# An AdaLN transformer block on one core: a weight load cut into four pieces, and six products moved from GpSimd to VectorE

## The chip, the cores and the metric

The kernel runs on one core of a Trainium2 chip. A core has five engines with an instruction queue each, worked off in order: TensorE (PE in the profile), VectorE (DVE), ScalarE (ACT), GpSimd (POOL) and SyncE (SP, which only issues transfers). The metric is the device time of one execution in microseconds; the figure for a kernel is the median of its runs.

## The reference

Two batches of 4096 rows of 512 values pass an attention-like block with a gated scan, and then a feed-forward block whose inputs and weights are rounded to FP4 in blocks of 16.

```python
mod = (silu(c) @ wmod).reshape(B, 6, 1, -1)
sa, ca, ga, sb, cb, gb = mod[:, 0], ..., mod[:, 5]
ga = sign(ga) * maximum(abs(ga), 0.25)          # gb the same
h = layernorm(x) * (1 + ca) + sa
# attention
xn = h / norm(h) * sqrt(512) * gamma
q, kv, a = split(xn @ W_qkva.T, 3);  a = sigmoid(a)
y[t] = a[t] * y[t - 1] + kv[t]                  # scan over the 4096 rows
x = x + ga * q * y
# feed-forward, fp4() rounds in blocks of 16
h = fp4(layernorm(x) * (1 + cb) + sb)
g = silu(h @ fp4(w_gate).T) * (h @ fp4(w_up).T)
x = x + gb * (fp4(g) @ fp4(w_down).T)
```

## The kernel before

**Stages.** The first stage (to about 564 us) is the attention part, the second the feed-forward part. The change lies in the opening of the first: the function `start` and slots 0 and 1 of the loop that follows.

**Tiles.** A token tile g is 128 rows; four of them make a block i of 512 rows. The 16 blocks are worked off in slots: slot = 4*i + e, where e counts the four groups of 128 output columns. In a slot, `mix(i, xT, e)` multiplies the block by the three parts of weight group e (`PARTS` = 2, 1, 0, which are a, kv and q), each in float16 high and low halves, 36 matmuls of 128x512 in all, into three banks of PSUM. Even e use banks 0 to 2 and odd e banks 3 to 5, so mix(0,2) writes the banks that mix(0,0) used. Block 0's first mix goes tile by tile instead, 36 matmuls of 128x128 for each of its four token tiles. The results of slot s are read in slot s+1: `gates` (sigmoid of bank one, on ScalarE), `scan` (VectorE), `read_out` (VectorE), `halves` and a transpose, and two slots later `joined` and `residual`.

**Token tiles.** Tile g goes through `norm_load`, `norm_moments`, `norm_stats` (VectorE, then rstd on GpSimd, L160 and L161), `norm_center` (L166), `norm_shift` (L172), `norm_square` (ScalarE, L354), `norm_gain` (rn on GpSimd, L359 and L361), `norm_hi` (ScalarE, L367) and `norm_lo` (VectorE, L372). `norm_lo` ends with a DMA transpose into xT, issued from SyncE. `start` does this for tiles 0 to 3; slot s does the high and low half of tile s+4 and prepares the next ones.

**Weight groups.** A group e has three parts of 128x512. For each: `load_part` (SyncE, 256 KB), `gamma_qkva` (times gamma, L281), `square_qkva` (sum of squares on ScalarE, L285), `inverse_qkva` (rs: VectorE L288, then a power on GpSimd L289), `hi_qkva` (L308 or L310) and `lo_qkva` (VectorE, L316, and a DMA transpose into wqT, L324). In short, (2,a), (2,b), (2,c) are the parts of group 2 in the order of `PARTS`. `gain_qkva` turns the sums into the gains `us` (L296 and L299). High and low halves of tiles and weights share a ring of four buffers `hl`; each comes free when its transpose has landed.

**Modulation.** Each of the six modulation vectors needs a 1 MB column block of `wmod`. Number 2 (`ga`) is loaded by `load_mod(2)`, multiplied in `mod_columns(2)` on TensorE after mix(0,0), and in slot 1 `signed_floor` (ScalarE L250; VectorE L251 to L253) and `prep_gain` (L563) make from it the factors gq that `read_out` uses.

**Order.** The source order is the order of each engine's queue: a manual schedule covers all engines. An instruction that waits holds up what is behind it on its engine. All loads and transposes of the opening are issued from SyncE, in one order:

```python
norm_lo(1, xT)
load_mod(2)            # one transfer of 1 MB
...
norm_lo(2, xT)         # transpose three
...
norm_lo(3, xT)         # transpose four
load_qkva(2)           # three transfers of 256 KB
```

Of the kernel before, what the change touches and what calls it, by code (L numbers as in the profile page):

```python
# [43 lines left out]
def tile_adaln_block(  # L44
# [165 lines left out]
    def load_mod(s, pieces=1):  # L210
        w = KC // pieces
        for k in range(0, KC, w):
            S.dma_start(
                wm[s][:, k : k + w, :],
                wmod[k * P : (k + w) * P, s * D : (s + 1) * D].rearrange("(k p) e -> p k e", p=P),
            )
# [109 lines left out]
    PARTS = (2, 1, 0)  # L326
# [17 lines left out]
    def norm_center(g):  # L344
        xh[g] = center(xld.pop(g), xstat[g][0], ca[g * P // N])
# [24 lines left out]
    def norm_lo(g, xT):  # L370
        h, rn, hl = xh.pop(g)
        V.scalar_tensor_tensor(  # L372
            out=hl[:, 1, :], in0=h, scalar=rn, in1=hl[:, 0, :], op0=ALU.mult, op1=ALU.subtract
        )
        t = g % KC
        S.dma_start_transpose(xT[:, :, t * P : (t + 1) * P], flat(hl))
# [270 lines left out]
    def start():  # L647
        a, b_, c_ = PARTS

        def load_mod_piece(s, k):  # L650
            S.dma_start(wm[s][:, k, :], wmod[k * P : (k + 1) * P, s * D : (s + 1) * D])

        load_mod(1, KC)
        norm_load(0)
        S.dma_start(gam, gamma.partition_broadcast(P))
        for k, then in enumerate((PARTS[0], PARTS[1], PARTS[2], None)):
            if then is None:
                norm_load(1)
            else:
                load_part(0, then)  # L660
            load_mod_piece(0, k)
        norm_load(2)
        norm_load(3)
        load_qkva(1)
        norm_load(KC)
        pc = mod_spread(1, 0)
        ps = mod_spread(0, 0)
        r1 = mod_rows(1)
        r0 = mod_rows(0)

        norm_moments(0)
        norm_stats(0)
        gamma_qkva(0, a, V)
        A.activation(ca[0], pc, AF.Copy, bias=1.0)
        square_qkva(0, a)
        gamma_qkva(0, b_, V)
        square_qkva(0, b_)
        inverse_qkva(0, a, a + 1)
        norm_center(0)
        gamma_qkva(0, c_, V)  # L680
        inverse_qkva(0, b_, b_ + 1)
        hi_qkva(0, a, True)
        square_qkva(0, c_)
        lo_qkva(0, a)
        inverse_qkva(0, c_, c_ + 1)
        hi_qkva(0, b_, True)
        norm_moments(1)
        norm_stats(1)
        lo_qkva(0, b_)
        A.copy(sa[0], ps)  # L690
        norm_center(1)
        hi_qkva(0, c_, True)
        norm_shift(0)
        norm_square(0)
        lo_qkva(0, c_)
        norm_gain(0, G)
        norm_shift(1)
        norm_square(1)
        norm_hi(0)
        norm_moments(2)  # L700
        norm_moments(3)
        norm_gain(1, G)
        norm_stats(2)
        norm_hi(1)
        norm_stats(3)
        norm_lo(0, xT)
        norm_center(2)
        norm_shift(2)
        norm_square(2)
        norm_lo(1, xT)  # L710
        load_mod(2)
        norm_gain(2, G)
        norm_center(3)
        norm_shift(3)
        norm_square(3)
        norm_gain(3, G)
        norm_hi(2)
        gamma_qkva(1, a, V)
        norm_lo(2, xT)
        norm_hi(3)  # L720
        gamma_qkva(1, b_, V)
        square_qkva(1, a)
        square_qkva(1, b_)
        norm_lo(3, xT)
        load_qkva(2)
        norm_load(KC + 1)
        inverse_qkva(1, b_, a + 1)
        gamma_qkva(1, c_, V)
        mod_store(*r1, tag="yh")
        square_qkva(1, c_)  # L730
        mod_store(*r0)
        hi_qkva(1, a, False)
        inverse_qkva(1, c_, c_ + 1)
        for part in PARTS:
            gamma_qkva(2, part)
        lo_qkva(1, a)
        hi_qkva(1, b_, True)
        norm_moments(KC)
        hi_qkva(1, c_, True)
        lo_qkva(1, b_)  # L740
        norm_stats(KC)
        lo_qkva(1, c_)
        norm_load(KC + 2)
        load_qkva(3)
        norm_center(KC)
        for part in PARTS:
            square_qkva(2, part)
        norm_shift(KC)
        norm_square(KC)
        norm_gain(KC, G)  # L750
        gain_qkva(0)
        norm_moments(KC + 1)
        inverse_qkva(2)
        norm_stats(KC + 1)
        for part in PARTS:
            hi_qkva(2, part, False)
            lo_qkva(2, part)
        gain_qkva(1)
        gain_qkva(2)
# [8 lines left out]
    with order:  # L768
        xT = new_xT()
        start()  # L770
        for slot in range(NS + 3):
            i, e = divmod(slot, KC)
            if e == 0 and slot < NS:
                if slot:
                    xT = nxT
                nxT = new_xT() if i + 1 < NBLK else None
            units, coming = coming, load_units(plan[slot]) if slot < len(plan) else []
            g = slot + KC
            if g + 3 < NT:
                norm_load(g + 3)  # L780
            cur = mix(i, xT, e) if slot < NS else None
            late = rows
            rows = None
            if slot == 0:
                cols = mod_columns(2)
            elif slot in MODS:
                rows = mod_rows(MODS[slot])
            if gate is not None:
                gate = gates(*gate)
            if len(joining) == 2 or slot >= NS + 2:  # L790
                residual(*joined(*joining.pop(0)))
            if g < NT:
                norm_hi(g)
            if gate is not None:
                gate = scan(*gate)
            if slot == 1:
                signed_floor(gq, cols, atile([P, KC, B], F32, "mag"))
                prep_gain(0)
            if g + 2 < NT:
                norm_moments(g + 2)  # L800
            if gate is not None:
                gate = read_out(*gate)
            if g < NT:
                norm_lo(g, nxT)
            if gate is not None:
                joining.append(halves(*gate))
            if slot == 1:
                for part in PARTS:
                    square_qkva(3, part)
            if g + 2 < NT:  # L810
                norm_stats(g + 2)
            for u in units:
                u.advance(1)
            if g + 1 < NT:
                norm_center(g + 1)
            for u in units:
                u.advance(2)
                u.advance(3)
            if g + 1 < NT:
                norm_shift(g + 1)  # L820
                norm_square(g + 1)
            if slot == 1:
                scale_qkva(3)
                for part in PARTS:
                    hi_qkva(3, part, False)
                    lo_qkva(3, part)
            for u in units:
                u.advance(4)
            coming = [Unit(*c_) for c_ in coming]
            for u in coming:  # L830
                u.advance(0)
            if g + 1 < NT:
                norm_gain(g + 1, G)
            if slot == 0:
                for part in PARTS:
                    gamma_qkva(3, part)
            for u in units:
                u.advance(5)
                u.advance(6)
            assert all(u.step == 7 for u in units)  # L840
            if 0 < slot < KC:
                prep_gain(slot)
            if slot + 2 in MODS:
                load_mod(MODS[slot + 2])
            if late is not None:
                mod_store(*late)
            if slot == KC + 1:
                ca[1] = mod_load(1, 1, "mod_c1")
                sa[1] = mod_load(0, 1, "mod_s1")
            if slot == NS // 2 + KC:  # L850
                mods_for(0)
            if slot == NS // 2 + KC + 2:
                gbs[0] = mod_load(5, 0, "mod_gb")
            if slot in (NS - 6, NS - 5):
                for n in range(2):
                    n += 2 * (slot - NS + 6)
                    x1s[n] = load_x1(n)
            if NS - 5 <= slot < NS - 1:
                n = slot - NS + 5
                xst[n] = stats_x(x1s[n])  # L860
                if n in (1, 2):
                    run(quant_x(n - 1, x1s.pop(n - 1), xst.pop(n - 1)))
            gate = cur
# [190 lines left out]
```

## Time and profile before

| | us |
|---|---|
| median of 3 runs (lowest to highest) | 1942.48 (1939.48 to 1942.65) |
| profiled execution, its own time | 1940.56 |
| its span | 1938.8 |
| TensorE busy | 1905.6 |
| VectorE busy | 1603.8 |
| ScalarE busy | 993.3 |
| GpSimd busy | 419.6 |

All times of instructions are from one profiled execution and count from the start of its span; around the span lie 1.8 us more. A line of the timeline gives start, busy time, engine, source line, what is written from what, how many, and in brackets the idle time of the engine ahead of it with what ended it. Starts of queued instructions on VectorE lie closer together than their busy times, since the end of one overlaps with the next. A transfer's row gives the time of its issue, not of its landing.

### The profile page before, as it was taken

To read this page: it belongs to the slowest core of one execution; us is meant where nothing else is said; L and a number is where in the kernel's file an instruction comes from. 1 tells how busy PE (TensorE), PEld (TensorE's weight loads), DVE (VectorE), ACT (ScalarE), POOL (GpSimd) and SP (SyncE) were. 2 spreads that over 40 slices of the span, in tenths; PEclk is the share of its full clock that TensorE was granted. 3 is DMA by queue.
4 is the path that set the end of the run, shared out by engine and by line. 5 is a ranking of instruction groups with operands and counts; after the bars stand their busy time and mean duration, and the time that the engine had idled before them with its cause. 6 is when DMAs were issued, how large, how long until landed. Compare 5 with 4: busy or idle time off the path is not lost.

```text
span 1938.8 us, 25685 instructions
## 1 busy us (share of the span) xinstructions
PE 1905.6 (98%) x9220; PEld 900.1 (46%) x9220; DVE 1603.8 (83%) x2671; ACT 993.3 (51%) x1705; POOL 419.6 (22%) x603
## 2 busy tenths in 40 slices
PE   7799999999999999999999999999999999999999
PEld 4344444444444444444444444444444444444444
DVE  5777889999859988888888888888888888888875
ACT  4544467777755454444445444444454444445432
POOL 4544466666530101000000000001001000000000
PEclk9999999999999999999999999999999999999999
DMA  8697679999833434433433344334434433433343
GB/s 228 157 238 199 170 166 204 220 203 198 189 93 63 94 63 76 81 63 63 80 77 63 67 81 83 63 74 84 68 63 78 79 63 63 82 75 63 61 69 58
DMA packets 483152, 206.66 MB, mean 107 GB/s; under 512 B 439574, under 2 KB 440854, under 8 KB 483024
## 3 DMA queue, kind: packets, MB, share of 16 engines
q1 hardware_dynamic: 468576, 171.50, 41.6%
q0 software_dynamic: 14448, 33.52, 9.8%
q8 instruction: 72, 1.18, 0.2%
q14 instruction: 56, 0.46, 0.1%
HBM read 63.12 MB, written 33.58 MB: 50 GB/s over the span
## 4 chain that ended last, share of the span: by engine, by line
PE 83%; DVE 2%; issue 1%; ACT 1%; DMA 0%; POOL 0%; ACTq 0%; POOLq 0%; DVEq 0%
PE mm L881 45%; PE sd L928 24%; PE mm L393 14%; DMA yt<-yh 0%; POOL xr L443 0%; DVE ld L172 0%; DVE xn L106 0%; DMA out_dram<-xr 0%; DVE xn L122 0%; POOL out_dram L445 0%; DVE y L420 0%; ACT y L435 0%; DVE hl L372 0%; DVE ld L166 0%; DVE hid L901 0%
## 5 line engine op out<-in xcount | busy, mean ns | idle before, releaser
L881 PEld LDWEIGHTS <-x2T 128*128 128x128 f16 x4608 | 450.9, 98 | 469.4 <-issue 1.3
L393 PE MATMUL mm<-xT,wqT 128*128 128x512 f16 (+1 forms) x2412 | 506.1, 373 | 20.4 <-DMA xT<-hl 9.5
L881 PE MATMUL mm<-wuT,x2T 128*128 128x512 f16 (+1 forms) x2304 | 487.7, 361 | 1.0 <-DVE hid L901 1.0
L881 PE MATMUL mm<-wgT,x2T 128*128 128x512 f16 (+1 forms) x2304 | 487.7, 361 | 0.0
L928 PE MATMUL sd<-wdT,hT 128*128 128x512 f16 x2112 | 465.8, 379 | 0.0
L393 PEld LDWEIGHTS <-wqT 128*128 128x128 f16 x2412 | 232.7, 99 | 295.4 <-issue 23.1
L928 PEld LDWEIGHTS <-hT 128*128 128x128 f16 x2112 | 206.6, 98 | 242.7
L896 ACT ACTIVATE silu<-mm,u 128x512 f32<-128x512 f32 (+1 forms) x192 | 125.1, 652 | 286.0 <-PE mm L881 282.4
L901 DVE SCALAR_TENSOR_TENSOR hid<-mm,u,silu 128x512 f32<-128x512 f32 (+1 forms) x192 | 128.5, 673 | 139.5 <-PE mm L881 130.4
L590 POOL TENSOR_SCALAR rstd<-vs 128x1 f32<-128x1 f32 x64 | 13.8, 216 | 983.9 <-ACT sq L588 983.9
L143 ACT ACTIVATE u<-ud,rms 128x1 f32<-128x1 f32 x64 | 19.0, 297 | 277.9 <-DVE rms L139 277.9
L120 ACT ACTIVATE sle<-sl 128x512 f16<-128x512 f32 (+2 forms) x162 | 147.2, 909 | 0.0
L113 ACT ACTIVATE she<-sh 128x1408 bf16<-128x1408 bf16 (+1 forms) x128 | 128.5, 1004 | 4.1
L952 POOL DMA_DIRECT2D out_dram<-o x63 | 56.3, 894 | 270.1 <-DVE o L946 266.2
L411 DVE TENSOR_TENSOR_SCAN y<-sig,cy,mm 128x512 f32<-128x512 f32 x56 | 71.7, 1280 | 46.3 <-ACT sig L405 17.4
L427 ACT COPY yh<-y 128x1024 uint16<-128x1024 uint16 x64 | 67.0, 1047 | 83.3 <-DVE y L420 75.2
L122 DVE SCALAR_TENSOR_TENSOR xn<-hid,xn 128x1408 f32<-128x1408 f32 x64 | 103.6, 1619 | 3.7 <-ACT hid L116 3.7
L106 DVE TENSOR_TENSOR xn<-hid,inv 128x1408 f32<-128x1408 f32 x64 | 104.0, 1625 | 2.2
L125 DVE SCALAR_TENSOR_TENSOR hhl<-hid,xn 128x1408 f16<-128x1408 f32 x64 | 104.0, 1625 | 2.2
L147 DVE TENSOR_REDUCE amh<-hid 128x88 f32<-128x1408 f32 x64 | 103.7, 1620 | 2.2
L116 ACT ACTIVATE hid<-xn 128x1408 f32<-128x1408 f32 x64 | 88.3, 1379 | 30.7 <-DVE xn L106 30.7
L443 POOL TENSOR_TENSOR xr<-xr,y 128x512 f32<-128x512 f32 x64 | 81.3, 1270 | 54.2 <-ACT y L435 52.8
(114 smaller groups left out, 1917.3 us busy)
## 6 DMA issues: line engine op xcount, KB each, us to landing
ld<-out_dram SPq DMA_DIRECT2D x65, 256.0 KB, 2.9
xr<-in_L_attn_x_dram SPq DMA_DIRECT2D x64, 256.0 KB, 3.5
out_dram<-xr POOLq DMA_DIRECT2D x64, 256.0 KB, 3.8
out_dram<-o POOLq DMA_DIRECT2D x63, 256.0 KB, 3.9
ld<-in_L_ffn_w_gate_dram SPq DMA_DIRECT2D x22, 256.0 KB, 3.2
ld<-in_L_ffn_w_up_dram SPq DMA_DIRECT2D x22, 256.0 KB, 3.3
scratch<-in_L_wmod_dram SPq DMA_DIRECT2D x4, 1024.0 KB, 5.5
ld<-in_L_ffn_w_down_dram SPq DMA_DIRECT2D x16, 256.0 KB, 3.2
```

The costliest lines, as they stand in the source:

```text
L106: V.tensor_tensor(blocks(xn), blocks(src), spread(inv, nb), ALU.mult)
L113: A.activation(blocks(she), spread(sh, nb), AF.Copy, scale=WPEAK)
L116: A.activation(a, xn, AF.Abs, scale=MAGIC)
L120: A.activation(blocks(sle), spread(sl, nb), AF.Copy, scale=WPEAK)
L122: V.scalar_tensor_tensor(out=xn, in0=a, scalar=FLOOR, in1=xn, op0=ALU.max, op1=ALU.add)
L125: V.scalar_tensor_tensor(out=nq, in0=a, scalar=FLOOR, in1=xn, op0=ALU.max, op1=ALU.subtract)
L147: V.tensor_reduce(am, src.rearrange("p (b k) -> p b k", k=QB), AX.X, ALU.max, apply_absolute_value=True)
L393: T.matmul(pp[:, t : t + width], wqT[:, wp * KC + k, r * P : (r + 1) * P], xT[:, xp * KC + k, t : t + width], start=n == 0, stop=n == 3 * ...
L881: T.matmul(pp[:, : n1 - n0], x2T[:, xp * KC + k, :], wt[:, wp * KC + k, n0:n1], start=n == 0, stop=n == 3 * KC - 1,)
L896: A.activation(sl[:, :w], pairs[j][0][:, :w], AF.Silu, scale=u[:, 0:1])
L901: V.scalar_tensor_tensor(out=hid[:, n0:n1], in0=pairs[j][1][:, : n1 - n0], scalar=u[:, 1:2], in1=sl[:, : n1 - n0], op0=ALU.mult, op1=ALU.mult,
L928: T.matmul(pd, hT[:, hp * IC + k, :], wdT[:, wd_chunk(wp, k), :], start=n == 0, stop=n == 3 * IC - 1,)
```

## The change

Three things change, all in the opening.

1. The 1 MB load of modulation weight 2 becomes four loads of 256 KB, one after each of the four x transposes; the three loads of weight group 2, which followed transpose four, go one each after transposes two, three and four.
2. The gamma products of group 2 move from GpSimd to VectorE and are put one at a time into VectorE's queue, each with its square on ScalarE; before, three stood together on GpSimd, and the squares stood ahead of `norm_shift` of tile 4.
3. The gamma products of group 3 (slot 0) move from GpSimd to VectorE at the same place in the text; their squares move in slot 1 from behind `halves` to ahead of `scan`.

```diff
--- before.py
+++ after.py
@@ -704,11 +704,13 @@
         norm_hi(1)
         norm_stats(3)
         norm_lo(0, xT)
+        load_mod_piece(2, 0)
         norm_center(2)
         norm_shift(2)
         norm_square(2)
         norm_lo(1, xT)
-        load_mod(2)
+        load_mod_piece(2, 1)
+        load_part(2, a)
         norm_gain(2, G)
         norm_center(3)
         norm_shift(3)
@@ -717,12 +719,15 @@
         norm_hi(2)
         gamma_qkva(1, a, V)
         norm_lo(2, xT)
+        load_mod_piece(2, 2)
+        load_part(2, b_)
         norm_hi(3)
         gamma_qkva(1, b_, V)
         square_qkva(1, a)
         square_qkva(1, b_)
         norm_lo(3, xT)
-        load_qkva(2)
+        load_mod_piece(2, 3)
+        load_part(2, c_)
         norm_load(KC + 1)
         inverse_qkva(1, b_, a + 1)
         gamma_qkva(1, c_, V)
@@ -731,23 +736,25 @@
         mod_store(*r0)
         hi_qkva(1, a, False)
         inverse_qkva(1, c_, c_ + 1)
-        for part in PARTS:
-            gamma_qkva(2, part)
         lo_qkva(1, a)
         hi_qkva(1, b_, True)
         norm_moments(KC)
         hi_qkva(1, c_, True)
         lo_qkva(1, b_)
+        gamma_qkva(2, a, V)
+        square_qkva(2, a)
         norm_stats(KC)
         lo_qkva(1, c_)
         norm_load(KC + 2)
         load_qkva(3)
         norm_center(KC)
-        for part in PARTS:
-            square_qkva(2, part)
+        gamma_qkva(2, b_, V)
+        square_qkva(2, b_)
         norm_shift(KC)
         norm_square(KC)
         norm_gain(KC, G)
+        gamma_qkva(2, c_, V)
+        square_qkva(2, c_)
         gain_qkva(0)
         norm_moments(KC + 1)
         inverse_qkva(2)
@@ -791,6 +798,9 @@
                 residual(*joined(*joining.pop(0)))
             if g < NT:
                 norm_hi(g)
+            if slot == 1:
+                for part in PARTS:
+                    square_qkva(3, part)
             if gate is not None:
                 gate = scan(*gate)
             if slot == 1:
@@ -804,9 +814,6 @@
                 norm_lo(g, nxT)
             if gate is not None:
                 joining.append(halves(*gate))
-            if slot == 1:
-                for part in PARTS:
-                    square_qkva(3, part)
             if g + 2 < NT:
                 norm_stats(g + 2)
             for u in units:
@@ -833,7 +840,7 @@
                 norm_gain(g + 1, G)
             if slot == 0:
                 for part in PARTS:
-                    gamma_qkva(3, part)
+                    gamma_qkva(3, part, V)
             for u in units:
                 u.advance(5)
                 u.advance(6)
```

No matmul, transpose or arithmetic is added or removed; SyncE issues three transfers more.

## The prediction

> **What bounds the kernel now.** I read the page first, then the waits, TensorE's timeline, and the queues of VectorE, GpSimd and SyncE, all between 20 and 90 us.
>
> ```profile
> PE 1905.6 (98%) x9220; PEld 900.1 (46%) x9220; DVE 1603.8 (83%) x2671; ACT 993.3 (51%) x1705; POOL 419.6 (22%) x603
> PE   7799999999999999999999999999999999999999
> ```
>
> TensorE is busy 1905.6 of 1938.8 us, and what is missing lies in the first two slices of 48.5 us. The diff touches only that opening, so what it can win is in TensorE's gaps there.
>
> ```profile
> 60.08 2.75 PE L393 MATMUL mm<-xT,wqT 128*128 128x512 f16 x12 [0.51 <-DVE y L420]
> 68.53 10.49 PE L393 MATMUL mm<-xT,wqT 128*128 128x512 f16 x36 [5.69 <-DMA wqT<-hl]
> 82.02 8.16 PE L393 MATMUL mm<-xT,wqT 128*128 128x512 f16 x37 [3.01 <-DMA xT<-hl]
> ```
>
> From 82.02 on (mix(1,0), slot 4) TensorE has no gap for over 160 us: whatever moves 82.02 moves the end. So the question is what 82.02 waits for. It is the transpose of the last x tile of block 1 (issued 77.60), which follows norm_lo in slot 3, which follows VectorE's queue of slots 2, 1 and the opening. The gap at 68.53 has the same source: the transposes of weight group 3, issued from 65.75, when lo_qkva(3) got its turn on VectorE. So VectorE's in-order queue from 36 to 68 us carries the end:
>
> ```profile
> 36.62 0.74 DVE L166 SCALAR_TENSOR_TENSOR ld<-xr,mv,ca 128x512 f32<-128x512 f32 x1
> 41.95 0.75 DVE L172 SCALAR_TENSOR_TENSOR ld<-ld,rstd,sa 128x512 f32<-128x512 f32 x1 [4.60 <-POOL rstd L161]
> ...
> 46.17 0.49 DVE L310 TENSOR_SCALAR hl<-scratch,rs 128x512 f16<-128x512 f32 x1 [2.57 <-POOL rs L289]
> ...
> 55.86 1.21 DVE L252 TENSOR_SCALAR mag<-mag 128x8 f32<-128x8 f32 x1
> 57.11 1.18 DVE L253 SCALAR_TENSOR_TENSOR gq<-gq,mag 128x8 f32<-128x8 f32 x1
> ...
> 63.31 0.17 DVE L288 TENSOR_SCALAR rs<-us 128x3 f32<-128x3 f32 x1 [1.20 <-ACT sq L285]
> ...
> 68.28 1.22 DVE L411 TENSOR_TENSOR_SCAN y<-sig,mm 128x512 f32<-128x512 f32 x1
> ```
>
> Each bracket is idle time ahead of the instruction and its releaser. GpSimd's queue explains the 4.60:
>
> ```profile
> 36.86 4.08 POOL L281 TENSOR_TENSOR scratch<-scratch,gam 128x512 f32<-128x512 f32 x3 [2.60 <-DMA scratch<-in_L_attn_W_qkva_dram]
> 41.03 0.23 POOL L160 TENSOR_SCALAR rstd<-mv 128x1 f32<-128x1 f32 x1
> ...
> 54.55 3.72 POOL L281 TENSOR_TENSOR scratch<-scratch,gam 128x512 f32<-128x512 f32 x3
> ```
>
> The three gamma products of group 2 wait for their weights until 36.86 and run until 40.94; rstd of tile 4, whose statistics were ready at 34.7, is queued behind them. The weights are late because SyncE's queue is:
>
> ```profile
> 26.60 0.57 SPq L213 DMA_DIRECT2D scratch<-in_L_wmod_dram  x1
> 29.06 4.75 SPq L376 DMA_TRANSPOSE xT<-hl  x2
> 33.86 1.52 SPq L208 DMA_DIRECT2D scratch<-in_L_attn_W_qkva_dram  x3
> ```
>
> Behind the 1 MB load the issue of transpose four took 3.41 us against 1.24 for others, and transpose three landed 6.0 us after its issue, at 35.1, against a shortest 2.7.
>
> **What the Trainium skill says.** "SBUF — State Buffer", Who interferes with whom: a VectorE instruction in a two-port mode, or with two SBUF inputs, contends with a GpSimd instruction that reads SBUF, and the second blocks. The trace agrees: L252 and L253 touch 8 elements and take 1.21 and 1.18 us while GpSimd's gamma products (1.26 each) run; L251, which reads PSUM, takes 0.17. "DMA: Bandwidth & Descriptors", Queues, rings and completion order: descriptors of one issuing queue are consumed in ring order, so a transpose waits for loads ahead of it; the 6.0 us landing fits. "TensorE: Matmul & The Clock Gate", Part 1: idle time halves the clock, by free-running windows of 3.41 us. The granted clock is 0.50 from 33 to 39 us and from 67 to 73, after gaps of 4.88 and 5.69; the gap of 3.01 left it at 1.00.
>
> **The change, part by part.** No matmul changes. Six products of 128x512 go from GpSimd (4.08+3.72 = 7.80 us) to VectorE (0.69 each; 0.61 from start to start). One load becomes four of 256 KB, three more issues of 0.45 us = 1.4 us on SyncE, but the three loads of group 2 now go between the transposes.
>
> SyncE: transposes one and two keep 22.78 and 25.3; transpose three is ready at 29.03 as before, now behind 512 KB, part of it moved. Its landing lies between 31.8 (shortest, 2.7) and 35.1 (as before); I take 33.0 (median 3.9). Transpose four then issues at about 31.25 and ends at 32.5; the last piece and the last part of group 2 at 33.4. That part, issued at 33.0, lands 3.2 us after its issue ends (the median of the six such loads from 20 to 85 us) at 36.6; with a repeat of the 3.41 us stall, 38.8.
>
> VectorE from 34.54 (end of lo_qkva(1,b)), in the new order, with spacings of the rows before:
> - gamma (2,a) 35.15; statistics 35.25; lo (1,c) 35.92. Its hi half needs the buffer that transpose three frees: before 35.15, now 33.0, so the 1.23 us wait goes.
> - center 36.58; gamma (2,b) 37.19; rstd is now ready by 36.3 to 37.1 (GpSimd 0.3+0.6, up to 0.6+1.05, after 35.4); shift ends 37.85, before 42.6.
> - gamma (2,c) 38.46; squares on ScalarE follow, the last ends 39.65 (0.73 to 0.8 each; norm_square goes ahead of it); rs at 39.8; GpSimd's rn, us, rs powers (0.3+0.55+0.85+0.85) from 39.0 to 41.55. hi (2,a) starts at **41.6, before 46.17: 4.6 earlier**. The 4.60 and 1.23 waits are gone, the 2.57 wait for rs stays at some 2, and three products (1.83) are added.
> - To the shift of tile 5 spacing is unchanged (5.87 from 46.17): 47.5. Then three gammas of group 3 to 50.0. Before, scan stood 2.18 after the shift, waiting for sig; now 2.5. Sig is at 49.0, so 0.3 is lost: 4.2 earlier.
> - gq: ScalarE now does three squares (0.81 each) between norm_hi and cy, mag: norm_hi 50.0, squares to 53.1, mag 53.2, L251 at 53.45, before 55.78. VectorE idles 2.1 us here: gain down to 2.3. But L252 and L253 lose their contention: about 0.5 from L251 to prep_gain instead of 2.55. Gain 4.4.
> - The 1.20 us wait for squares at 63.31 is gone; next late is GpSimd, where rs now stands behind rstd until 58.15 (before 62.54). hi (3,a) at 59.05, before 64.45: **5.4 earlier**. Then as before: scan at 62.9, first transpose of group 3 at 60.4, mix(0,3) at 63.2, mix(1,0) at 76.6.
>
> TensorE does not limit this: even at its old 44.81 mix(0,1) ends at 52.74; mix(0,2) needs the bank that read_out frees at about 55.5 and ends near 58.3, before mix(0,3) at 63.2. The idle gap there, 4.9, still costs half clock, but as before it is covered by the wait for xT. SyncE's 1.4 us of issue lie in the stretch where its stall shrinks. GpSimd's loss of 7.8 us of work costs nothing.
>
> Sum: -5.4 us on the profiled execution (1940.56, span 1938.8) gives 1935.2. The median of the runs is 1942.48, 1.9 above the profiled one, inside their 1939.48 to 1942.65; the same -5.4 gives **1937.1**. About 0.2% (3.9 us) is what a measurement of this kernel can tell from no change.
>
> **Rivals.**
> 1. The last part of group 2 comes late: gamma (2,c) blocks VectorE, with shift's successors behind it. The price is landing minus 37.85: 1.0 with one stall of the 3.41 kind (38.8), 2.5 with the slowest landing of such loads, 7.3 us after 33.0. Gain 2.9 to 4.4, some **1939.0**. For it: the opening's loads landed in up to 7.3. Against: less is queued ahead of each transpose.
> 2. The clock falls in the gap before mix(1,0): that costs about 5 us at half clock, 2.5 us (36 matmuls took 10.49 at 68.53 against 7.93 at 44.81). It needs mix(0,3) to end well before xT lands, so a warm start at 63.2; the 4.9 us gap speaks against. **1939.6**.
> 3. The chain is not what I read and the gain goes into another wait (sig or the gq wait of 2.1 growing): **1942.5**, within 0.2%.
> 4. The slow side: every transpose put behind a load pays 2.17 us more issue (3.41-1.24), as transpose four did. Three such before the last part (6.5) bring it to 43.1, eating nearly all 5.4; three more on the transposes of group 1 hold the hl buffers that hi (2,c) and norm_hi(4) need, which adds up to 4: **1946**. It decides from some three stalls on to no gain, five to slower. Against it: transposes behind four loads at 35.95 took 4.67 for three, only 0.95 over.
>
> **How the numbers follow.** Main 0.66 (gain 4 to 7: 1935.5 to 1938.5), first rival 0.14, second 0.09, third 0.05, fourth 0.06. Half of the first counts as faster and half as same, a little of the second faster: faster 0.74, same 0.19, slower 0.07. The range reaches down to 9 gained (5.4, some 1.0 where GpSimd's powers take their short ends, and 2.6 for the spread of the runs, whose lowest lies 3.0 under the median) and up to 1.5 gained (the worse end of the first rival, 2.9, with 1.4 of spread): 1933.5 to 1941.0. It leaves out rivals three and four.
>
> **What would show it.** In the profile after: no GpSimd L281 rows; shift of tile 4 near 38 and hi (2,a) near 41.6; L252 and L253 near 0.2; VectorE waiting about 2 us for mag; mix(0,3) near 63 and mix(1,0) near 76.6. It is wrong if hi (2,a) stays past 45, a gamma (2,c) wait over 2 us appears, or mix(1,0) starts past 80.

## The result, and the profile after

| | before | after |
|---|---|---|
| median of 8 runs each, us (lowest to highest) | 1941.77 (1939.48 to 1942.65) | 1935.99 (1934.53 to 1936.86) |
| ratio to before, 95% interval | | 0.9971, 0.996 to 0.9982 |
| profiled execution, its own time / span | 1940.56 / 1938.8 | 1934.53 / 1932.8 |

The kernel became 5.8 us faster, and the slowest run of after lies 2.6 below the fastest of before. 1937.1 had been forecast, 5.4 below the median of the three runs known then.

On the page of after, the engines' busy times and TensorE's 40 slices:

```profile
PE 1905.7 (99%) x9220; PEld 899.6 (47%) x9220; DVE 1605.6 (83%) x2677; ACT 991.0 (51%) x1705; POOL 415.2 (21%) x597
PE   7899999999999999999999999999999999999999
```

TensorE's work is what it was (1905.7 against 1905.6). Six instructions went from GpSimd to VectorE (603 to 597, 2671 to 2677), and the second slice rose from 7 to 8. So the span lost idle time, most of it in the opening. TensorE's timeline of after from 20 us on (start, busy, line, count, and in brackets the idle time ahead and what ended it) shows how much:

```profile
33.63 2.91 PE L393 MATMUL mm<-xT,wqT 128*128 128x128 f16 x36 [2.92 <-DMA xT<-hl]
...
63.69 10.54 PE L393 MATMUL mm<-xT,wqT 128*128 128x512 f16 x36 [4.66 <-DMA wqT<-hl]
76.92 8.36 PE L393 MATMUL mm<-xT,wqT 128*128 128x512 f16 x38 [2.69 <-DMA xT<-hl]
```

33.63 is the token tile that transpose three brings. mix(0,3) starts at 63.69 where it started at 68.53, and mix(1,0) at 76.92 where it started at 82.02: 5.10 us of the span's 6.0. VectorE's timeline of after tells where the 5.10 was won:

```profile
37.74 0.75 DVE L172 SCALAR_TENSOR_TENSOR ld<-ld,rstd,sa 128x512 f32<-128x512 f32 x1 [0.46 <-POOL rstd L161]
38.99 0.69 DVE L281 TENSOR_TENSOR scratch<-scratch,gam 128x512 f32<-128x512 f32 x1 [0.50 <-DMA scratch<-in_L_attn_W_qkva_dram]
...
42.12 0.49 DVE L310 TENSOR_SCALAR hl<-scratch,rs 128x512 f16<-128x512 f32 x1 [1.34 <-POOL rs L289]
...
54.04 0.17 DVE L251 TENSOR_SCALAR gq<-sd 128x8 f32<-128x8 f32 x1 [2.36 <-ACT mag L250]
54.12 0.16 DVE L252 TENSOR_SCALAR mag<-mag 128x8 f32<-128x8 f32 x1
54.32 0.17 DVE L253 SCALAR_TENSOR_TENSOR gq<-gq,mag 128x8 f32<-128x8 f32 x1
...
59.59 0.49 DVE L310 TENSOR_SCALAR hl<-scratch,rs 128x512 f16<-128x512 f32 x1 [1.00 <-POOL rs L289]
```

Line by line against before: the shift of tile 4 (L172) waits 0.46 us for rstd, no longer 4.60. Gamma (2,c) waits 0.50 for its weights: the new wait that the first rival feared, and small. hi (2,a) starts at 42.12, before 46.17. The wait of 2.36 for mag is new: ScalarE has the three squares of group 3 first. L252 and L253 take 0.16 and 0.17 us where they took 1.21 and 1.18. hi (3,a) starts at 59.59, before 64.45.

The other 0.9 us lie far from the change. Later on the same timeline TensorE has a gap at about 250 us in both kernels. Before had one more at 377.94, in slot 40, here with its bracket:

```profile
377.94 186.64 PE L393 MATMUL mm<-xT,wqT 128*128 128x512 f16 x864 [0.85 <-ACT cy L414]
```

After has none there: its row of 1440 matmuls (576 + 864) runs through it.

```profile
245.68 312.65 PE L393 MATMUL mm<-xT,wqT 128*128 128x512 f16 x1440 [2.31 <-ACT y L435]
```

### The profile page after: what moved, and what is told of

It is laid out like the page before. It is cut to its first block, busy times and chain, and to the rows that moved or that the text cites. A ratio compares the mean times of both kernels' runs of the same rounds, so it can differ in the third digit from the quotient of the medians.

```text
span 1932.8 us, 25689 instructions
## 1 busy us (share of the span) xinstructions
PE 1905.7 (99%) x9220; PEld 899.6 (47%) x9220; DVE 1605.6 (83%) x2677; ACT 991.0 (51%) x1705; POOL 415.2 (21%) x597
## 3 DMA queue, kind: packets, MB, share of 16 engines
q8 instruction: 72, 1.18, 0.3%
## 4 chain that ended last, share of the span: by engine, by line
PE 87%; DVE 0%; issue 0%; ACT 0%; POOL 0%; ACTq 0%
PE mm L888 47%; PE sd L935 24%; PE mm L393 16%; ACT y L435 0%; DVE o L953 0%; DVE o L964 0%; DVE ld L172 0%; DVE st L153 0%; DVE hl L372 0%; DVE y L420 0%; DVE ld L166 0%; DVE hid L908 0%; ACT sig L405 0%; ACT sq L354 0%; DVE inv L100 0%
```

## The experiments

The theory: the gain is VectorE's queue in the opening, as the prediction has it, and comes from parts 2 and 3 (gamma products of group 2, of group 3). Two rivals: that the loads and the earlier transposes (part 1) bring it, and that the contention on L252 and L253 alone does. The first five kernels do parts alone or undo one; s1 moves the loads; b1 and b3 go on to the wait that the change had made; the f kernels test a later gap that turned out to take gains back. Ratios are to before, run on the same chip. Starts of different executions are not exactly comparable: the first x transpose, which stands ahead of everything that the edits move, is issued between 22.03 us (e2) and 22.94 us (b1). The table at the end of this section gives it for each, and where it matters a start is counted from there as well.

### One part alone: e1, e2, e3

e1, part 1 on the kernel before:

```diff
         norm_lo(0, xT)
+        load_mod_piece(2, 0)
...
         norm_lo(1, xT)
-        load_mod(2)
+        load_mod_piece(2, 1)
+        load_part(2, a)
...
         norm_lo(3, xT)
-        load_qkva(2)
+        load_mod_piece(2, 3)
+        load_part(2, c_)
```

> Before, with part 1 of the change alone: the modulation load in pieces and the loads of group 2 between the transposes; all gamma products stay on GpSimd. Theory V (VectorE's queue carries the end, through GpSimd's products): the products start at about 34.4 instead of 36.86, but the last waits for its weights until 39.0, so rstd of tile 4 is free at about 40.4 instead of 41.03; hi (2,a) some 0.7 us earlier, the whole 0.3 to 1.5 us faster. Rival T (the gain is in the x transposes and TensorE's first mix, which the loads release): this part alone gives most of it, 4 us or more.

Measured: 1941.05 against 1940.82, ratio 1.0002 (0.9994 to 1.001). hi (2,a) came at 45.09 where before had 46.17, and mix(1,0) at 81.41 where it had 82.02, of which 0.2 us is left when counted from the first x transpose. The loads alone bring nothing that the times show, less than was expected; slot 40 has a gap of 1.66 where before has 0.85 (the last experiments are about it).

e2, part 2 on the kernel before:

```diff
-        for part in PARTS:
-            gamma_qkva(2, part)
...
         lo_qkva(1, b_)
+        gamma_qkva(2, a, V)
+        square_qkva(2, a)
...
-        for part in PARTS:
-            square_qkva(2, part)
+        gamma_qkva(2, b_, V)
+        square_qkva(2, b_)
...
         norm_gain(KC, G)
+        gamma_qkva(2, c_, V)
+        square_qkva(2, c_)
```

> Before, with the products of group 2 on VectorE, loads as before. Theory V: gamma (2,a) waits for its late weights until 36.9 and (2,b), (2,c) follow without a wait, so hi (2,a) is at about 43.3 (before 46.17, after 42.12); 2.9 us faster than before. L252 and L253 still take 1.2 each. Rival T: about no gain (under 1), since the transposes stay late. Rival C (the gain is the removed contention between the two engines on L252 and L253): no gain.

Measured: 1939.62, ratio 0.9993 (0.9985 to 1.0001), less than half of what was expected. Yet hi (2,a) was at 43.01, 3.2 us earlier, and mix(1,0) on e2's TensorE timeline 3.6 us earlier (2.9 counted from the first x transpose, which is what theory V had):

```profile
78.39 41.83 PE L393 MATMUL mm<-xT,wqT 128*128 128x512 f16 x180 [5.10 <-DMA xT<-hl]
```

The opening did what it should and the end did not follow. The row says why: the same 180 matmuls took 39.13 in before (39.01 in after) and take 41.83 here, after a gap of 5.10. The clock had fallen in the gap, which took 2.8 us back. The view by stretches has it at half behind the gap (stretch, its length, TensorE busy with its matmuls, granted clock, DMA share, GB/s):

```profile
78.00:82.00 4.00, 3.61 (x9) 0.50 0.58 157
```

e3, part 3 on the kernel before:

```diff
+            if slot == 1:
+                for part in PARTS:
+                    square_qkva(3, part)
             if gate is not None:
                 gate = scan(*gate)
...
             if slot == 0:
                 for part in PARTS:
-                    gamma_qkva(3, part)
+                    gamma_qkva(3, part, V)
```

> Before, with the products of group 3 on VectorE and their squares ahead of scan; group 2 and the loads as before. Theory V: L252 and L253 fall from 1.2 to 0.2 each, but mag comes some 2.2 us later behind the squares, so prep_gain stays near 58.4; only the 1.2 us wait for the squares at rs goes, and rs then stands behind rstd: hi (3,a) 0.9 us earlier, 0.9 us faster. Rival C: 2 us or more faster. Rival T: no gain.

Measured: 1940.07, ratio 0.9996 (0.9987 to 1.0004). L252 and L253 took 0.16 and 0.17, and the new wait for mag was 2.36, as in after. mix(1,0) started 1.6 us earlier (1.0 counted from the first x transpose), and a fall of the clock behind its gap of 3.57 us took 1.86 back. So the contention can be taken away whole, with the wait for mag that comes with it, and at most 1.6 of after's 5.1 us follow: as the cause of the gain, that rival falls. What the contention would be worth without the wait for mag, e3 does not show.

### One part undone: e4, e5

e4, after without part 3:

```diff
-            if slot == 1:
-                for part in PARTS:
-                    square_qkva(3, part)
             if gate is not None:
                 gate = scan(*gate)
...
                 joining.append(halves(*gate))
+            if slot == 1:
+                for part in PARTS:
+                    square_qkva(3, part)
...
-                    gamma_qkva(3, part, V)
+                    gamma_qkva(3, part)
```

> After, with the products of group 3 back on GpSimd and their squares back behind halves (parts 1 and 2 of the change alone). Theory V: L252 and L253 take 1.2 each again, while the wait for mag goes from 2.36 to under 0.5; prep_gain about where it is in after (54.5); the squares end near 59.4, so rs waits for them and hi (3,a) comes 0.8 us later: 0.5 to 1.2 us slower than after, that is 4.6 to 5.3 faster than before. Rival C: 2 us or more slower than after.

Measured: 1938.47, ratio 0.9988 (0.9981 to 0.9994): 2.4 us faster than before, half of what was expected. By the ratios that is 3.3 us slower than after, which is where rival C had put it; the median alone does not tell the two apart, the trace does. mix(1,0) starts at 77.07, 0.15 later than in after, and 0.9 later counted from the first x transpose, as theory V had it (0.5 to 1.2). VectorE's timeline of e4 shows the contention back, the wait for mag gone, and a wait for the squares in its place:

```profile
51.07 1.22 DVE L252 TENSOR_SCALAR mag<-mag 128x8 f32<-128x8 f32 x1
52.32 1.18 DVE L253 SCALAR_TENSOR_TENSOR gq<-gq,mag 128x8 f32<-128x8 f32 x1
...
58.51 0.17 DVE L288 TENSOR_SCALAR rs<-us 128x3 f32<-128x3 f32 x1 [1.19 <-ACT sq L285]
```

In after that L288 stands at 58.22, which is 1.1 us earlier when both are counted from the first x transpose: about the wait for the squares. The other two effects of part 3 nearly cancel: 2.1 us of contention go (1.22 + 1.18 to 0.16 + 0.17), and the wait for mag grows by 2.0 (from 0.34 in e4 to 2.36). What else e4 lost in this execution, it lost at slot 40, by its TensorE timeline:

```profile
374.37 188.33 PE L393 MATMUL mm<-xT,wqT 128*128 128x512 f16 x864 [2.41 <-DMA xT<-hl]
```

A gap of 2.41, and the 864 matmuls behind it took 1.69 us longer than before's 186.64: 4.1 us together. f1, further down, has e4's opening without that gap, and its ratio of 0.9977 is 1.2 us from after's: rival C has no support in it.

e5, after without part 1:

```diff
-        load_mod_piece(2, 0)
...
-        load_mod_piece(2, 1)
-        load_part(2, a)
+        load_mod(2)
...
-        load_mod_piece(2, 3)
-        load_part(2, c_)
+        load_qkva(2)
```

> After, with the modulation load in one piece of 1 MB and the loads of group 2 behind transpose four, as before (parts 2 and 3 of the change alone). Theory V: gamma (2,a) waits for its weights until about 36.9 (34.60 in after), lo (1,c), center and shift stand behind it; hi (2,a) at about 43.3 instead of 42.12, and the end 1.1 us later than after, 4.6 faster than before. Rival T: most of the gain is gone, 3 us or more slower than after.

Measured: 1936.57, ratio 0.9975 (0.9965 to 0.9984), as expected, though hi (2,a) came at 44.14 and not at 43.3. By the medians nearly the whole gain is there without the new order of loads; with e1, the rival that the loads bring it falls. Parts 2 and 3 alone had given 1.2 and 0.8 us by their medians (both intervals take in 1), together they give 4.5. Some of that difference is what was lost on the way: by the table at the end of this section e2 and e3 lose 1.9 us each more than before does after the start of mix(1,0), e5 only 0.7 more. The rest the single profiles do not show. What part 1 adds to parts 2 and 3 is open: 0.8 us by the ratios (0.9975 to 0.9971), well inside the intervals, but 2.2 us in the two profiled executions, where mix(1,0) starts at 78.75 here and at 76.92 in after (counted from the first x transpose). e5's profiled execution was its slowest, and gamma (2,a), now on VectorE, started at 36.78 in it and at 34.60 in after: late weights hold up VectorE's queue itself once the products stand there.

### Transposes behind loads: s1

s1 is after with the four modulation pieces behind transpose four; the parts of group 2 stay between the transposes.

```diff
         norm_lo(0, xT)
-        load_mod_piece(2, 0)
...
         norm_lo(3, xT)
-        load_mod_piece(2, 3)
         load_part(2, c_)
         norm_load(KC + 1)
+        for k in range(KC):
+            load_mod_piece(2, k)
```

> After, with all four pieces of the modulation load behind transpose four and the next x load; the parts of group 2 stay between the transposes. It asks why transposes three and four land late (4.5 us after the issue in after, 6.0 in before, shortest 2.7). If they wait for the bytes loaded ahead of them, transpose three, with only one load of 256 KB ahead of it, lands within 3.2 us and no SyncE issue between 28 and 36 us takes over 1.3 us. If it is a pause of the queue at this place whatever is loaded, transpose three still takes 4 us or more and some issue takes 1.7 us or more. TensorE's first mix has room, so theory V expects the end within 1.5 us of after: what may come later are the transposes of group 1, behind 1 MB.

Measured: one run, 1937.37. The four x transposes and their landings, from the answers on line 376 in the opening of before, after and s1, in this order:

```profile
DMA to landing us min/median/max: 2.7/4.3/6.0
```

```profile
DMA to landing us min/median/max: 2.7/3.6/4.5
```

```profile
DMA to landing us min/median/max: 2.7/3.1/3.7
```

Neither forecast came out whole: the slowest landing of 3.7 us lies between their 3.2 and 4, and one issue took 2.08, where the first allowed 1.3. But the fewer bytes stand ahead of the transposes, the sooner they land, and the other executions repeat it: the slowest landing is 5.7 to 6.2 us in the four with the 1 MB load (before, e2, e3, e5) and 4.5 to 5.2 in the nine with after's order. So a late landing goes with the load ahead; what lengthens an issue stays open. The x transposes of after take 1.25 us at most to issue where one of before took 3.41, and in s1 one of 2.08 is there, though only 256 KB stand directly ahead of it.

### The wait for mag: b1, b3

The 2.36 us wait for mag is the largest left on VectorE's queue. b1 is after with the squares of group 3 behind the instructions that need mag:

```diff
-            if slot == 1:
-                for part in PARTS:
-                    square_qkva(3, part)
             if gate is not None:
                 gate = scan(*gate)
             if slot == 1:
                 signed_floor(gq, cols, atile([P, KC, B], F32, "mag"))
                 prep_gain(0)
+                for part in PARTS:
+                    square_qkva(3, part)
```

> After, with the squares of group 3 behind signed_floor and prep_gain of slot 1 instead of ahead of scan, so that cy and mag on ScalarE no longer stand behind them. Theory V: VectorE's wait of 2.36 us for mag goes almost entirely (mag follows cy, near 51.8), everything behind it moves up by 2.0, and the squares end near 54.5, ahead of rs: 1.5 to 2.2 us faster than after. If something else than VectorE's queue sets mix(1,0): no change.

Measured: 1933.94, ratio 0.9963 (0.9951 to 0.9975), as expected. By the ratios that is 1.6 us faster than after (2.1 by the medians), with overlapping intervals. VectorE's timeline of b1:

```profile
51.95 0.17 DVE L251 TENSOR_SCALAR gq<-sd 128x8 f32<-128x8 f32 x1 [0.33 <-ACT mag L250]
...
57.51 0.49 DVE L310 TENSOR_SCALAR hl<-scratch,rs 128x512 f16<-128x512 f32 x1 [1.00 <-POOL rs L289]
```

The wait is down to 0.33 and hi (3,a) stands 2.08 earlier than in after. mix(1,0) starts at 74.96, 1.96 earlier, behind a gap of 3.72. The view by stretches shows the price (columns as for e2):

```profile
76.00:79.00 3.00, 3.00 (x8) 0.50 0.49 121
```

TensorE is busy all 3 us at half clock; after, in the first 3 us of its own mix(1,0), from 77 on, does 15 matmuls at 1.00.

b3 takes the same instructions out of slot 1 altogether:

```diff
             if slot == 0:
+                signed_floor(gq, cols, atile([P, KC, B], F32, "mag"))
+                prep_gain(0)
                 for part in PARTS:
                     gamma_qkva(3, part, V)
...
-            if slot == 1:
-                signed_floor(gq, cols, atile([P, KC, B], F32, "mag"))
-                prep_gain(0)
...
+            if slot == 1:
+                inverse_qkva(3)
             if g + 2 < NT:
                 norm_stats(g + 2)
...
-                scale_qkva(3)
+                gain_qkva(3)
```

> After, with signed_floor and prep_gain(0) moved from slot 1 to the end of slot 0, ahead of the gamma products of group 3 (mod_columns has ended by 43.1), and inverse_qkva(3) ahead of norm_stats in slot 1, so that rs does not stand behind rstd on GpSimd. Theory V: the wait for mag (2.36) goes, 0.8 us of gq work moves ahead of the products, and the wait for rs falls from 1.0 to about 0: hi (3,a) at about 56.5 instead of 59.59, mix(1,0) near 74; 2.4 to 3.4 us faster than after. The gap ahead of mix(0,3) falls from 4.66 to about 2.

Measured: 1936.11, ratio 0.9974 (0.9965 to 0.9983): no faster than after, though mix(1,0) started at 73.95, 3.0 us earlier (2.3 counted from the first x transpose). Two items ate it: the 180 matmuls took 40.70, 1.7 more, and slot 40 had a gap of 2.37.

### The gap at slot 40: f1 to f4

In slots 36 and 38 SyncE issues broadcast loads of modulation vectors (L267), ahead of the transposes for slot 40. SyncE's timeline of e4 there:

```profile
348.07 1.04 SPq L267 DMA_DIRECT2D mod<-modd  x2
...
352.14 3.86 SPq L429 DMA_TRANSPOSE yt<-yh  x1
...
365.83 0.57 SPq L267 DMA_DIRECT2D mod<-modd  x1
...
367.46 2.08 SPq L376 DMA_TRANSPOSE xT<-hl  x1
```

These two transposes behind them took 3.86 and 2.08 us to issue. So the edit moves the loads to slots 52 and 54, nearer to where their values are first used: f1 is e4 with it, f2 is b3, f3 is b1, and f4 is e4 unchanged.

```diff
-            if slot == NS // 2 + KC:
+            if slot == NS - 12:
                 mods_for(0)
-            if slot == NS // 2 + KC + 2:
+            if slot == NS - 10:
                 gbs[0] = mod_load(5, 0, "mod_gb")
```

> As e4 (parts 1 and 2 of the change), with the broadcast loads of the modulation rows of the second stage, which SyncE issues in slots 36 and 38 (L267), moved to slots 52 and 54. The profile of e4 has a TensorE gap of 2.41 us at 374 us (slot 40) that after has not, and SyncE's transposes around those loads take 2 to 4 us to issue. Theory M (those loads slow the queue and the xT of block 10 comes late): the gap at slot 40 is gone or under 0.3, a new one may stand at slot 56; if none does, some 2 us faster than e4. Rival L (the gap is a lottery of the execution and has nothing to do with those loads): the gap stays in about half of the looks and the median stays within 0.5 us of e4.

> As b3, with the same loads moved from slots 36 and 38 to 52 and 54. b3 started mix(1,0) at 73.95, 3.0 us earlier than after, and was not faster; its profile has a gap of 2.37 us at slot 40. Theory M: that gap goes, and b3 becomes 2 us or more faster, some 1934. Rival L: no change.

> As b1, with the same loads moved. b1 had no gap at slot 40. Theory M: no change from b1 (within 0.7 us) if no new gap stands at slot 56. Rival L: the same.

> e4 unchanged, one more look. If the gap at slot 40 belongs to this kernel, it is there again with 2 us or more; if it is a lottery of the execution, it may be anything from 0 to 2.5. The start of mix(1,0) should be within 0.5 us of the 77.07 of the first look.

| kernel | median, us | ratio, 95% interval | gap at slot 40 |
|---|---|---|---|
| e4 | 1938.47 | 0.9988 (0.9981 to 0.9994) | 2.41, in f4 1.22 |
| f1 | 1937.15 | 0.9977 (0.997 to 0.9984) | none |
| b3 | 1936.11 | 0.9974 (0.9965 to 0.9983) | 2.37 |
| f2 | 1933.35 | 0.9964 (0.995 to 0.9977) | none |
| b1 | 1933.94 | 0.9963 (0.9951 to 0.9975) | none |
| f3 | 1934.35 | 0.9966 (0.9954 to 0.9979) | none |

f4, a single run of the same kernel as e4, took 1937.87. Its mix(1,0) started at 78.56, 1.5 us after e4's and not within the 0.5 expected: 0.7 of that stands between their first x transposes already. Between 340 and 378 us the slowest landing of an x transpose is 6.6 to 7.6 us in the eleven executions with the loads in slots 36 and 38, and 5.2 or 5.3 in the three without. On TensorE's timeline of f2 the row runs through:

```profile
244.53 312.57 PE L393 MATMUL mm<-xT,wqT 128*128 128x512 f16 x1440 [2.55 <-ACT y L435]
```

Where the gap was, the edit removes it, and the ratio falls by 0.0011 (e4 to f1) and 0.0010 (b3 to f2), about 2 us; where there was none, b1, it does nothing. No gap appears at slot 56 instead. The two pairs point one way, but the intervals of each pair overlap. These loads are therefore a likely part of the cause, not all of it: after, e5, s1 and b1 have the same loads in the same slots and no gap, and f4 shows that the gap changes from one execution to the next. What decides its size stays open.

### All executions in one sum

With these rows the profiles can be closed. Beside the issue of the first x transpose the table takes the start of mix(1,0), the excess of its first 180 matmuls over 39.01, the excess behind the gap at about 250 us (over e2's 124.48 for 576 matmuls; over 310.96 for 1440, which is after's 312.65 less the 1.69 between 126.17 and 124.48), and the gap at slot 40 with the excess behind it (over 186.64). The last column is the start of the first feed-forward matmuls that wait, near 590 us, less all of these but the first x transpose.

| kernel | first x transpose | mix(1,0) starts (gap ahead) | excess there | excess at 250 | slot 40 | rest |
|---|---|---|---|---|---|---|
| before | 22.78 | 82.02 (3.01) | 0.12 | 1.69 | 0.85 | 512.0 |
| after | 22.86 | 76.92 (2.69) | 0 | 1.69 | 0 | 511.8 |
| e1 | 22.38 | 81.41 (3.27) | 0 | 1.69 | 1.66 | 512.0 |
| e2 | 22.03 | 78.39 (5.10) | 2.82 | 0 | 1.70 | 512.2 |
| e3 | 22.21 | 80.43 (3.57) | 1.86 | 1.69 | 1.03 | 512.2 |
| e4 | 22.08 | 77.07 (3.06) | 0 | 1.69 | 2.41 + 1.69 | 512.2 |
| f4 | 22.82 | 78.56 (3.22) | 0 | 1.65 | 1.22 | 512.1 |
| e5 | 22.53 | 78.75 (3.44) | 1.70 | 1.69 | 0 | 511.9 |
| s1 | 22.45 | 77.06 (4.91) | 2.63 | 1.77 | 0 | 511.8 |
| b1 | 22.94 | 74.96 (3.72) | 1.69 | 0.04 | 0 | 511.7 |
| b3 | 22.21 | 73.95 (3.46) | 1.69 | 1.69 | 2.37 | 512.3 |
| f1 | 22.32 | 78.26 (3.82) | 1.85 | 1.69 | 0 | 512.0 |
| f2 | 22.53 | 73.97 (5.07) | 1.56 | 1.61 | 0 | 512.1 |
| f3 | 22.45 | 75.45 (4.94) | 2.30 | 1.69 | 0 | 511.8 |

The rest is the same within 0.6 us, and so is what follows to the end of the span (1342.0 to 1342.6), so no other place takes or gives more than that.

**Where a gap costs the clock.** Each trace records when the granted clock changed. Within one execution all these changes lie a whole number of windows of 3.413 us apart, and a stretch at half clock lasts one, two or three windows; from one execution to the next this grid lies elsewhere against the kernel. So the windows can be taken one by one (columns as for e2). In after, the edge at 75.8 us cuts the gap ahead of mix(1,0) in two and the clock stays up, while the gap at about 250 (here 243.4 to 245.7) lies inside one window, behind which the clock is at half:

```profile
72.40:75.80 3.40, 1.83 (x9) 1.00 0.70 150
75.81:79.22 3.41, 2.30 (x11) 1.00 0.68 160
...
243.06:246.47 3.41, 1.10 (x6) 1.00 1.12 202
246.48:249.88 3.40, 3.40 (x10) 0.50 0.49 141
```

In e2 an edge cuts the gap of 2.25 at 250, and the clock stays up:

```profile
247.96:251.37 3.41, 1.45 (x7) 1.00 1.30 193
251.38:254.78 3.40, 3.40 (x17) 1.00 0.76 138
```

From 46 us to the end of the program, in all 14 traces, the clock fell behind each of the 32 windows in which it was up and TensorE was busy for 38% or less, and behind none of those with 40% or more. It came back behind windows that were busy for 93% or more, and not behind those with 68% or less. By these figures, as an estimate, a single gap of under 2.0 us in a dense stretch costs only itself, one of over 4.3 us always costs the clock as well, and between them it depends on where the gap lies on the grid.

Each row of the table is one execution, and e4 and f4, the same kernel, start mix(1,0) 1.5 us apart; the medians carry the verdicts, and the rows say where time can go.

## Why the prediction was right, point by point

**The bound.** That the end hangs on VectorE's queue of the opening is shown: parts 2 and 3 without part 1 keep 0.9975, part 1 without them 1.0002, and in b1 a wait on that queue shorter by 2.03 us brings mix(1,0) 1.96 earlier.

**SyncE.** Transpose three was put at 33.0 and its tile started on TensorE at 33.63, behind an idle gap of 2.92 us. No x transpose stalled, but a piece of the modulation load did, which the sum had at 0.45 us, and the last part of group 2 came late. SyncE's timeline of after:

```profile
30.41 1.77 SPq L651 DMA_DIRECT2D scratch<-in_L_wmod_dram  x1
...
34.99 0.44 SPq L208 DMA_DIRECT2D scratch<-in_L_attn_W_qkva_dram  x1
```

That last part was put at 33.0 and at 36.6 on landing; it was issued at 34.99 and landed 4.0 us later, at 38.99. (The view counts a landing from the start of the issue; the sum had counted its 3.2 us from the end.) So this step was off by 2.4 us and the first rival's 38.8 was nearly right. It cost next to nothing in this execution: the shift ahead of gamma (2,c) was itself half a microsecond late, so gamma (2,c) waited 0.50, and hi (2,a) hung on GpSimd. That is in part luck. In e4, f2, b3, f1, f4 and f3, with the same order of loads and the same products on VectorE, this wait was 0.53, 0.92, 1.04, 1.14, 1.67 and 1.78 us, in b1 hardly any. Stalls of the fourth rival's kind came later: of the three transposes of group 2, issued from 43.42, one took 3.15 us where those of before took 1.26 at most, but mix(0,2), which needs them, followed mix(0,1) without a gap.

**hi (2,a)** was put at 41.6 and came at 42.12. Of the 0.5, 0.46 is the wait for rstd: GpSimd's power (L161) took 1.52 us there, and the step had allowed 0.6 to 1.05.

**gq.** L251 was put at 53.45 and came at 54.04; the wait for mag was put at 2.1 and was 2.36. The contention went as said, 1.21 and 1.18 to 0.16 and 0.17.

**hi (3,a) and mix.** 59.05 against 59.59, mix(0,3) 63.2 against 63.69, mix(1,0) 76.6 against 76.92. The delay of half a microsecond from hi (2,a) is carried along and partly lost again. The sum was -5.4 and -5.10 is what the start shows. That the medians differ by 5.8 is closer to the forecast than the sum can claim: slot 40, which it did not have, and the spread among the runs (3.2 us before, 2.3 after) are in it.

**The step that was incomplete** is "whatever moves 82.02 moves the end". For after it held, since its gap of 2.69 left the clock at 1.00; that was in part luck, since with one and the same opening e4 and f4 kept the clock there and f1 lost it. For e2 it didn't: 3.6 us at the start were 2.8 less behind it. The second rival had the mechanism right, and about the price (2.5 forecast, 1.6 to 2.8 measured at this place), but a condition that is not needed: f1 lost 1.85 behind a mix(0,3) that was itself slow (36 matmuls in 10.19, against 7.93 at full clock). The gap at slot 40 stood in no case of the prediction, and its 0.85 is most of the 0.9 by which the span fell more than the start.

**GpSimd's loss of 7.8 us of work** cost nothing, as said: its queue, 21% busy, makes tile 4 wait 0.46 us for rstd, no longer 4.60.

What was not won is the wait for mag, which the sum had named (2.1 lost): b1 puts the squares behind it, for a median of 1933.94. f2 has the lowest, 1933.35; the intervals of b1, f2 and f3 overlap with after's, so neither their order nor that they beat after is settled.

## What to carry to other kernels

A product on an engine with time to spare is not free if short instructions queue behind it there and the limiting engine waits for them; moving 1.83 us of it onto the limiting queue cut a wait of 4.60 to 0.46. A gain at the start of a long busy stretch must be followed to the end of the program: here falls of the clock behind gaps and a gap at slot 40, 300 us later, cost e2 4.5 us, where they cost before 2.7. Where one profile is the evidence, close the sum over all gaps before crediting a difference to an edit.

## What the runs showed of the hardware that had not been expected

- Whether a gap costs the clock is not decided by its length alone. Ahead of mix(1,0), gaps of 2.69 to 3.27 us kept it and gaps of 3.44 to 5.10 lost it, but gaps of 2.20 to 2.63 at 250 us lost it in all executions of the table except e2 and b1 (2.25 and 2.18), and at slot 40 a gap of 2.41 lost it and one of 2.37 did not. The Trainium skill, "TensorE: Matmul & The Clock Gate", Part 1, describes free-running windows of 3.41 us; the traces agree, since in all 14 executions every change of the clock lies on a grid of 3.413 us. By the same Part 1 it takes an idle window to lower the clock; here a window 38% busy lowered it, and one 40% busy did not. The usual price, 1.69 us, is half of 3.4: one window at half clock.
- GpSimd's power of one value per partition (L161) took 0.57 us with VectorE idle beside it (before, at 41.35) and up to 1.52 while VectorE ran products of two inputs (after, at 36.19).
- A DMA transpose's issue on SyncE, 1.23 us at the shortest, took up to 4.36 us behind loads in the same queue (one of the group 2 transposes of s1), and behind others no longer than alone.
